# The product of a layer-1 block behind the next block's sums, and at most five gathers in flight

## The chip, the cores and the metric

The kernel runs on one core of a Trainium2 chip. The time is the device time of one execution in microseconds (us). Three runs of the kernel before gave 2042.39, 2044.34 and 2052.66, a median of 2044.34. One more execution was profiled.

The engines of the core are named as in the profile: PE (TensorE, matrix products), DVE (VectorE), ACT (ScalarE), POOL (GpSimd, which here mostly issues gathers and scatters), SP (SyncE, which only issues plain transfers). Each engine has its own queue of instructions and works through it in order; engines wait for one another on semaphores.

## The reference, cut to what matters

```python
def _L1_gnn_ref(input, adj, W, a1, a2):
    h = input @ W
    f1 = h @ a1
    f2 = h @ a2
    e = leaky_relu(f1 + f2.T, negative_slope=0.2)
    scores = where(adj > 0, e, NEG)
    attention = softmax(scores, axis=1)
    return relu(attention @ h)

x = _layernorm(x + layer0(x, adj, ...))
x = _layernorm(x + _L1_gnn_ref(x, adj, W, a1, a2))
```

Two graph-attention layers follow each other over 2708 nodes with 1024 features, both with a residual and a layer norm. The adjacency matrix is sparse: a bit under 0.6% of it is ones. Layer 0 has the same shape with other scores (`relu(f @ g.T)`); the change leaves it as it is.

## The kernel before

**Lists.** The kernel first turns each row of the adjacency matrix into a list of neighbours (up to line 449). The nodes are ordered by the number of neighbours and cut into 22 blocks of 128 (the one numbered 0 holds what is left over). A block has up to four groups of 32 nodes, and each group's lists are cut into tiles: a tile holds 128 neighbour rows, four for each of the 32 nodes. In layer 1 the blocks run in the order of their tile counts: 3, 15, 15, 16, 16 and then 17 blocks of 20 tiles, 405 in all. The text counts them as k = 0 to 21.

**Layer 0** (lines 774 to 1009) leaves its normed output in two DRAM tensors: `X1S`, for the residual, and the table `T1` (`T` in the profile), whose rows are the 1024 features and four more columns, the first of which is the score term f2. A row is 1028 floats, so that a gather of 128 rows moves 526,336 bytes.

**Layer 1** (lines 1012 to 1126) uses that attention @ (x W) = (attention @ x) W: it first sums the gathered rows with the attention's weights and then multiplies the sum of the block by the weight matrix M, which stays in SBUF. For a block k:

- *Gathers.* POOL issues one indirect DMA for each tile into a ring of 32 slots (20 in `ring`, 12 in `more`). The class `Layer` (line 642) keeps the order. A slot is gathered into again once the sums have read it. This happens at three marks inside `Layer.sums`: after 4 tiles, after 12, and after the last. At each mark the gathers for all slots freed since are put into POOL's queue together.
- *Scores.* `scores1` on DVE picks the f2 column out of the landed tiles, adds f1, applies the leaky ReLU and the mask; `Layer.soft` takes the maximum, has ACT do the Exp, and builds `st`, the weights spread into 128x32 matrices, and `rs`, their sums.
- *Sums.* `Layer.sums` runs small matmuls on `rs` (their reciprocal is `ri`), then for each tile two half-width matmuls with a 128x32 weight into the PSUM tile `po`, four column groups of the array side by side. In the profile they read `po<-ring,st 128*32` and `po<-more,st 128*32`, and a block of 20 tiles has 40 of them, which the profile records as some 80. Then ACT scales the sums: `y<-po,ri`, two instructions.
- *Turn and product.* `turn` (line 517) transposes y on PE with eight transposes (`pt<-ident,y`) and ACT copies them to `yT`. `product` (line 535) multiplies `yT` by M in 32 recorded matmuls (`pm<-M,yT`) into the PSUM tile `pm`. For block 0, which has few rows, `split_product` puts four parts of the product side by side in column groups of the array and adds them with a second product.
- *Close.* `close1` loads the residual with SP's queue, adds the ReLU of `pm` to it on DVE (`z<-pm` or `u2b<-pm`, the two buffers of the result), norms it (`bst`, `newton` and so on; ACT's `z<-z,sh,rstd`), and scatters it to the output on POOL. The scatter is issued by a *hook*: the function handed to the next block's `sums` with a tile's number, here 6.

The order of work on each engine is the program order: the wrapper `InOrder` (line 61) ties every instruction to the one before it on its engine, and a scheduler may not move it. Dependencies through tiles become semaphore waits. Each gather or scatter of POOL takes one of eight DMA semaphores in turn, and so waits for the one eight back.

So before the change the PE order in layer 1 is: sums(k), transposes(k), product(k), rs(k+1), sums(k+1). ACT's order is y(k), the yT copies(k), Exp(k+1), z(k). Accumulators in PSUM are one `po`, two `pm` and two `pt`.

Of the kernel before, what the change touches and what calls it, by code (L numbers as in the profile page):

```python
# [106 lines left out]
def listed_path(ctx, tc, x, adj, Wf, bf, Wg, bg, W, bW, W1, a1, a2, out):  # L107

    nc = tc.nc
    P = 128  # L110
# [3 lines left out]
    TW = D + 4  # L114
    NB = (N + P - 1) // P
# [62 lines left out]
        nc.gpsimd.memset(t, 0.0)  # L178

    def gather(engine, dst, table, idx, rows=N):  # L180
        engine.indirect_dma_start(
            out=dst, out_offset=None, in_=table,
            in_offset=bass.IndirectOffsetOnAxis(ap=idx, axis=0), bounds_check=rows - 1, oob_is_err=False)

# [350 lines left out]
    def product(n, xT, w, row=None):  # L535


        pm = ps_m.tile([P, H, 512], F32, name="pm")
        for h in range(H):
            half_product(pm, h, n, xT, w, row)  # L540
        return pm
# [9 lines left out]
    def two_products(n, xT, w, row=None):  # L551

        halves = [ps_m.tile([P, H, 512], F32, name="pm") for h in range(H)]
        for h in range(H):
            half_product(halves[h], h, n, xT, w, row)
        return halves
# [23 lines left out]
    def whole(steps):  # L580

        while True:
            try:
                next(steps)
            except StopIteration as end:
                return end.value
# [54 lines left out]
    class Layer:  # L641

        def __init__(self, units, rings, width, table, stp, batched):
            self.units, self.table, self.width, self.stp, self.batched = units, table, width, stp, batched

            self.first = {g: i for i, g in enumerate(g for u in units for g in u.gs)}
            self.slots = [(t, i) for t in rings for i in range(t.shape[1])]
            self.count = len(self.slots)  # L650
            self.order = [(u, g, t) for u in units for _, g, t in u.tiles]
            assert all(self.first[g] < NSL0 for _, g, _ in self.order[:self.count])
            self.next, self.free, self.most = 0, set(), len(self.order)
# [9 lines left out]
        def gathers(self, latest=None):  # L663
            ready = []
            while self.next < min(self.most, len(self.order)) and (self.next < self.count or self.next - self.count in self.free):
                ready.append(self.next)
                self.next += 1
            if latest is not None and latest + self.count in ready:
                ready.remove(latest + self.count)
                ready.insert(0, latest + self.count)  # L670
            for m in ready:
                u, g, t = self.order[m]
                idx = SL[:, g, t:t + 1] if m >= self.count else SL0[:, self.first[g], t:t + 1]
                gather(pool, self.rows(m), self.table, idx)

        def soft(self, u):

# [97 lines left out]
    with ExitStack() as s0s:  # L775
# [155 lines left out]
        for k, u in enumerate(units):  # L931
            nxt = units[k + 1] if k + 1 < len(units) else None
            b = u.b
# [77 lines left out]

    with ExitStack() as s1s:
        new_pool = lambda name, bufs: s1s.enter_context(tc.tile_pool(name=name, bufs=bufs))
        tp, yp, zp, ovp = (new_pool(n, 1) for n in ("tp1", "yp1", "zp1", "ovp"))
        stp = new_pool("stp1", 2)

        x1 = [rb, u1b]
        z1 = [u2b, zp.tile([P, D], F32, name="z1")]
        more = new_pool("ring1", 1).tile([P, R1 - R0, TW], F32, name="more")

        order1 = sorted(range(NB), key=lambda b: (sum(TILES[g] for g in groups[b]), b))
        units = cut(R1, Q, order1)
        lay = Layer(units, [ring, more], TW, T1[:, :], stp, True)
        done1 = {b: i for i, b in enumerate(order1)}
        for u in units:
            g, at = u.gs[0], lay.first[u.gs[0]]
            if u.at < lay.count:
                dve.tensor_scalar(SL0[:, at:at + u.G], SL[:, g:g + u.G, :], float(N - 1), None, op0=ALU.min)


        fq = ovp.tile([P, NB, Q], F32, name="fq")
        f1q = ovp.tile([P, NB, Q], F32, name="f1q")
        dve.tensor_tensor(fq, f1.unsqueeze(2).to_broadcast([P, NB, Q]), quad.unsqueeze(1).to_broadcast([P, NB, Q]),
                          op=ALU.mult)
        pt = ps_t.tile([P, 4, P], F32, name="pt")
        pe.matmul(pt[:, 0, :Q * NB], rep, fq.rearrange("p b q -> p (b q)"), start=True, stop=True)
        dve.tensor_copy(f1q.rearrange("p b q -> p (b q)"), pt[:, 0, :Q * NB])

        def scores1(u):
            for k, g in enumerate(u.gs):  # L1040
                at = [lay.slots[(u.at + m) % lay.count] for m, tile in enumerate(u.tiles) if tile[0] == k]
                t0 = 0
                while t0 < len(at):

                    t, s = at[t0]
                    step = at[t0 + 1][1] - s if t0 + 1 < len(at) and at[t0 + 1][0] is t else 0
                    c = 1
                    while step > 0 and t0 + c < len(at) and at[t0 + c][0] is t and at[t0 + c][1] == s + c * step:
                        c += 1
                    dve.tensor_scalar(u.sc[:, k, t0:t0 + c], t[:, s:s + (c - 1) * step + 1:max(step, 1), D],  # L1050
                                      f1q[:, u.b, k:k + 1], None, op0=ALU.add)
                    t0 += c
            dve.scalar_tensor_tensor(u.sc, u.sc, SLOPE, u.sc, op0=ALU.mult, op1=ALU.max)
            dve.tensor_add(u.sc, u.sc, masked(u))
            lay.soft(u)

        def close1(b, pm):
            m, xt, z = valid[b], x1[done1[b] % 2], z1[done1[b] % 2]
            sp.dma_start(xt[:m], X1S[start[b]:start[b] + m, :])
            last = b == order1[-1]  # L1060

            def add(h):
                c = slice(h * 512, (h + 1) * 512)
                dve.scalar_tensor_tensor(z[:m, c], pm[h][:m, h, :], 0.0, xt[:m, c], op0=ALU.max, op1=ALU.add)

            if not last:
                dve.scalar_tensor_tensor(z[:m], flat(pm)[:m], 0.0, xt[:m], op0=ALU.max, op1=ALU.add)
            for _ in norm(z, m, add if last else None):
                pass
            yield  # L1070
            scatter(out, ids[:m, b:b + 1], z[:m])


        over = ovp.tile([P, NG, QT], F32, name="over")

        def mark_over(b):

            for g in groups[b]:
                if g == 0:
                    for q in range(Q):  # L1080
                        pool.memset(over[32 * q:32 * q + valid[0], 0, TILES[0]:], 1.0)
                elif TILES[g] < QT:
                    pool.memset(over[:, g, TILES[g]:], 1.0)

        def count_over():
            dve.scalar_tensor_tensor(over, SL, float(N), over, op0=ALU.is_lt, op1=ALU.mult)
            dve.tensor_reduce(bad[:, 0:1], over, AX.XY, ALU.add)
            dve.tensor_reduce(bad[:, 0:1], bad, AX.X, ALU.add)
            pt = ps_t.tile([P, 4, P], F32, name="pt")
            pe.matmul(pt[0:1, 0, 0:1], bad[:, 0:1], ones, start=True, stop=True)  # L1090
            act.copy(flag, pt[0:1, 0, 0:1])

        lay.gathers()
        pool.memset(over, 0.0)
        scores1(units[0])
        closing = iter(())
        for k, u in enumerate(units):
            b = u.b
            po = ps_s.tile([P, H, 512], F32, name="po")
            y = yp.tile([P, D], F32, name="y1")  # L1100
            lay.sums(u, po, {6: [lambda s=closing: [None for _ in s]]}, y)
            yT = tp.tile([P, KC, P], F32, name="yT")
            for _ in turn(y, nrows[b], yT, halves=True):
                pass

            if k + 1 == NB:
                prod = two_products(P, yT, M)
            elif b > 0:
                prod = product(P, yT, M)
            else:  # L1110
                prod = whole(split_product(yT, M, z1[1]))
            for i in (2 * k, 2 * k + 1):
                if i < NB:
                    mark_over(i)
            if k == NB // 2 + 1:
                count_over()
            if k + 1 < NB:
                scores1(units[k + 1])
            closing = close1(b, prod)
            if k + 1 < NB:  # L1120
                next(closing)
            if k + 2 == NB:
                unfit = nc.values_load(flag[0:1, 0:1])
        for _ in closing:
            pass
    return unfit

# [362 lines left out]
```

## Time and profile before

| | |
|---|---|
| median of three runs | 2044.34 us (2042.39 to 2052.66) |
| profiled execution | 2036.4 us, span in the trace 2034.6, mean granted PE clock 0.902 |
| layer 1 in it | from about 1220 us to the end |
| busy in the span: PE, DVE, ACT, POOL | 1634.2, 1169.8, 641.6, 1193.3 us (80, 57, 32, 59%) |
| mean DMA rate | 247 GB/s |
| layer 1's gathers | 260 into `ring`, mean 1002 ns on POOL, and 145 into `more`, mean 999 ns |
| product with M in layer 1 (`pm<-M,yT`) | 704 matmuls, 327.5 us |
| the sums of both layers (`po<-ring,st`) | 2660 matmuls, 333.5 us |
| ends of the sums of k = 4, 5, 20, 21 | 1360.67, 1389.74, 1971.12, 2003.47 us |

A line of the profile's timeline gives the start, the duration, the engine, the source line (here that of a helper, L71, for all), the operation, what it writes and reads, the shapes, the number of instructions taken together, and in brackets the engine's idle time before it and what ended it. "remote" or "another core or an unknown queue" means that the wait's releaser could not be found in the records. Of a waits list the columns are the total, the number of waits and the longest. A stretch of the windows table gives, for each engine, the busy time and the number of instructions, and then the granted PE clock (1.00 is full), the mean busy share of the 16 DMA engines, and the rate.

### The profile page before, as it was taken

Reading aid. Unit: us, or ns where it says so; the run is one execution under the profiler, and the core shown is the slowest. Engines: PE = TensorE matmul, PEld = TensorE weight load, DVE = VectorE, ACT = ScalarE, POOL = GpSimd, SP = SyncE. Lnnn points to the kernel's source line nnn. Section 1 sums busy time; section 2 is a strip of 40 time slices with the busy share of each in tenths; the row PEclk is TensorE's granted clock in tenths of the full one; section 3 lists DMA queues with packets and bytes.
Section 4 is the critical chain, followed back from the end, with each engine's and each line's share of the span. In section 5 each row is a group of like instructions: output and inputs, shape, how many; then the busy total and the mean of one; then the engine's idle time right before and its main releaser. Section 6 shows DMA issues by size and latency. Waiting matters only on the chain.

```text
span 2034.6 us, 22766 instructions
## 1 busy us (share of the span) xinstructions
PE 1634.2 (80%) x7313; PEld 686.3 (34%) x7313; DVE 1169.8 (57%) x3539; ACT 641.6 (32%) x861; POOL 1193.3 (59%) x1192
## 2 busy tenths in 40 slices
PE   5998569889999999999999963887657776657766
PEld 3443223333434434443434420332223232223222
DVE  6879447867878888888888751332231332222322
ACT  4545326444444455544455410110110110110110
POOL 7877545746656667666666416655555555555540
PEclk9999779989989999999999986998878878878878
DMA  7644545746867668877678728877788778888760
GB/s 276 242 170 149 179 159 206 268 165 249 300 239 284 243 234 280 295 283 279 232 245 297 300 97 340 297 274 287 261 294 279 266 266 290 278 279 286 261 222 23
DMA packets 149981, 502.25 MB, mean 247 GB/s; under 512 B 32468, under 2 KB 32500, under 8 KB 147144
## 3 DMA queue, kind: packets, MB, share of 16 engines
q0 software_dynamic: 132032, 427.76, 59.5%
q1 hardware_dynamic: 10202, 55.72, 7.5%
q10 hardware_dynamic: 7618, 17.23, 2.4%
q8 instruction: 59, 0.97, 0.2%
q14 instruction: 70, 0.57, 0.1%
HBM read 509.64 MB, written 33.75 MB: 267 GB/s over the span
## 4 chain that ended last, share of the span: by engine, by line
PE 21%; DVE 9%; another core or an unknown queue 9%; issue 7%; DMA 2%; POOL 2%; ACT 2%; ACTq 1%; POOLq 0%; DVEq 0%
PE pm L71 17%; DVE j L71 2%; PE pt L71 2%; PE po L71 2%; DVE newton L71 2%; DVE bst L71 1%; POOL ring L71 1%; DVE rstd L71 1%; DMA ring<-T,SL 1%; DVE z L71 1%; ACT y L71 1%; DMA ring<-in_x_dram,SL 1%; ACTq L71 1%; DVE u2b L71 1%
## 5 line engine op out<-in xcount | busy, mean ns | idle before, releaser
L71 POOL DMA_INDIRECT ring<-in_x_dram,SL x405 | 437.6, 1081 | 308.7 <-issue 97.3
L71 DVE SCALAR_TENSOR_TENSOR j<-ring,Fr 128x1024 bf16<-128x1024 f32 x402 | 495.2, 1232 | 95.3 <-DMA ring<-in_x_dram,SL 61.0
L71 POOL DMA_INDIRECT ring<-T,SL x260 | 260.6, 1002 | 207.8 <-PE po L71 111.0
L71 ACT COPY Fr<-pm 32x1024 f32<-32x1024 f32 (+2 forms) x353 | 340.8, 965 | 20.9 <-issue 11.9
L71 PE MATMUL pm<-M,xT 128*128 128x512 f32 x672 | 323.8, 630 | 22.1 <-issue 22.0
L71 PE MATMUL po<-ring,st 128*32 128x512 f32 x2660 | 333.5, 606 | 0.2 <-PE pt L71 0.2
L71 PE MATMUL pm<-M,yT 128*128 128x512 f32 (+1 forms) x704 | 327.5, 644 | 6.3 <-issue 4.2
L71 PE MATMUL pm<-Wt,xT 128*128 128x512 f32 (+1 forms) x704 | 305.3, 599 | 3.4 <-issue 3.2
L71 PE MATMUL pt<-ident,y 128*128 128x128 f32 (+1 forms) x352 | 62.7, 334 | 202.1 <-ACT y L71 188.2
L71 POOL DMA_INDIRECT more<-T,SL x145 | 144.9, 999 | 117.4 <-PE po L71 64.8
L71 PEld LDWEIGHTS pm<-M,yT 128*128 128x128 f32 (+1 forms) x704 | 138.2, 204 | 183.2 <-issue 177.6
L71 PEld LDWEIGHTS pm<-M,xT 128*128 128x128 f32 x672 | 130.6, 199 | 200.0 <-issue 200.0
L71 PEld LDWEIGHTS pm<-Wt,xT 128*128 128x128 f32 (+1 forms) x704 | 124.7, 186 | 157.6 <-issue 157.0
L71 PEld LDWEIGHTS po<-ring,st 128*32 128x32 f32 x2660 | 98.1, 112 | 185.4 <-issue 185.0
L409 POOL TENSOR_TENSOR adj<-adj,iota 128x2708 f32<-128x2708 f32 (+3 forms) x23 | 130.5, 5684 | 24.1 <-ACT adj L71 24.0
L71 ACT ACTIVATE y<-po,ri 128x512 f32<-128x512 f32 (+1 forms) x88 | 55.9, 684 | 250.1 <-remote 166.9
L71 ACT ACTIVATE scores<-scores 128x24 f32<-128x24 f32 (+5 forms) x44 | 10.0, 227 | 390.4 <-DVE scores L71 234.2
L71 PEld LDWEIGHTS pt<-ident,y 128*128 128x128 f32 (+1 forms) x352 | 50.5, 172 | 236.2 <-ACT y L71 208.6
L412 DVE MAX8 cand<-adj 128x8 f32<-128x136 f32 (+2 forms) x440 | 97.3, 285 | 36.5 <-POOL adj L409 36.5
L71 ACT ACTIVATE z<-z,sh,rstd 128x1024 f32<-128x1024 f32 (+1 forms) x31 | 38.5, 1241 | 245.1 <-DVE sh L71 244.9
L71 PE MATMUL pm<-halfT,WfT 128*128 128x512 f32 x256 | 113.9, 600 | 1.1 <-ACT WfT L71 1.1
L71 DVE TENSOR_SCALAR scores<-ring,f1q 128x4 f32<-128x4 f32 (+4 forms) x98 | 21.3, 240 | 155.5 <-DMA ring<-T,SL 124.1
(201 smaller groups left out, 1490.7 us busy)
## 6 DMA issues: line engine op xcount, KB each, us to landing
adj<-in_adj_dram SPq DMA_DIRECT2D x21, 1354.0 KB
X1S<-z SPq DMA_DIRECT2D x19, 512.0 KB
ring<-in_x_dram,SL POOLq DMA_INDIRECT x405
u1b<-X1S SPq DMA_DIRECT2D x11, 512.0 KB
rb<-X1S SPq DMA_DIRECT2D x10, 512.0 KB
ring<-T,SL POOLq DMA_INDIRECT x260
rows<-in_L_gnn_Wg_dram ACTq DMA_DIRECT2D x8, 512.0 KB
rows<-in_L_gnn_Wf_dram ACTq DMA_DIRECT2D x8, 512.0 KB
```

Of the source, the lines that this page charges most:

```text
L71: made = self.tc.keep_in_program_order(op(*args, **kwargs))
L409: nc.gpsimd.tensor_tensor(k[:n, cut], k[:n, cut], iota[:n, cut], op=ALU.mult)
L412: nc.vector.max(cand[:n, s, :], k[:n, s * SEG:min((s + 1) * SEG, N)])
```

## The change

Two things change, both in layer 1 alone.

1. *The order.* The product of a block is issued behind the next block's sums. PE's order becomes sums(k), product(k-1), transposes(k), rs(k+1), sums(k+1). `yT` is kept from one iteration to the next in the dictionary `turned`, and its pool has two buffers. `next(steps)` issues the transposes; the yT copies on ACT now come behind `scores1(k+1)`, so behind the Exp. `close1(k-1)` follows that. The scatter's hook moves from tile 6 to tile 12 of the sums, which puts it behind the gathers of the second mark in POOL's queue, and it belongs to the block before. Block 0 (k = 0) still runs its split product in its own iteration. After the loop come the product of k = 21 and the closings of the last two blocks; the product of k = 20 has come behind the sums of k = 21.
2. *The limit.* `Layer` has a new argument `flight`, 5 for layer 1 and none for layer 0. Every gather gets a dependency on the gather five ahead of it, so that POOL waits until that one has landed before it issues the next.

The number of instructions on each engine is the same.

```diff
@@ class Layer
-        def __init__(self, units, rings, width, table, stp, batched):
+        def __init__(self, units, rings, width, table, stp, batched, flight=None):
+            self.flight, self.issued = flight, []
...
-                gather(pool, self.rows(m), self.table, idx)
+                made = gather(pool, self.rows(m), self.table, idx)
+                if self.flight is not None:
+                    if len(self.issued) >= self.flight:
+                        tc.add_manual_dep(
+                            made.ins, self.issued[-self.flight],
+                            mybir.DependencyInfo(mybir.DependencyClass.Sync, mybir.DependencyReason.DATA),
+                            reason="gathers in flight")
+                    self.issued.append(made.ins.name)
@@ layer 1
-        tp, yp, zp, ovp = (new_pool(n, 1) for n in ("tp1", "yp1", "zp1", "ovp"))
-        stp = new_pool("stp1", 2)
+        yp, zp, ovp = (new_pool(n, 1) for n in ("yp1", "zp1", "ovp"))
+        stp, tp = (new_pool(n, 2) for n in ("stp1", "tp1"))
...
-        lay = Layer(units, [ring, more], TW, T1[:, :], stp, True)
+        lay = Layer(units, [ring, more], TW, T1[:, :], stp, True, 5)
...
+        turned = {}
         for k, u in enumerate(units):
...
-            lay.sums(u, po, {6: [lambda s=closing: [None for _ in s]]}, y)
+            lay.sums(u, po, {12: [lambda s=closing: [None for _ in s]]}, y)
+            closing = iter(())
+            prods = {c: product(P, turned.pop(c), M) for c in list(turned)}
             yT = tp.tile([P, KC, P], F32, name="yT")
-            for _ in turn(y, nrows[b], yT, halves=True):
-                pass
-
-            if k + 1 == NB:
-                prod = two_products(P, yT, M)
-            elif b > 0:
-                prod = product(P, yT, M)
+            steps = turn(y, nrows[b], yT, halves=True)
+            next(steps)
+            if b == 0:
+                for _ in steps:
+                    pass
+                prods[b] = whole(split_product(yT, M, z1[1]))
             else:
-                prod = whole(split_product(yT, M, z1[1]))
+                turned[b] = yT
...
+            if k + 1 < NB:
+                scores1(units[k + 1])
+            for _ in steps:
+                pass
             if k == NB // 2 + 1:
                 count_over()
-            if k + 1 < NB:
-                scores1(units[k + 1])
-            closing = close1(b, prod)
-            if k + 1 < NB:
+            for c, pm in prods.items():
+                closing = close1(c, pm)
                 next(closing)
...
+        prod = two_products(P, turned.pop(b), M)
         for _ in closing:
+            pass
+        for _ in close1(b, prod):
             pass
```

More of the change, by code (lines that the diff above doesn't have):

```diff
@@ L180, in gather @@
     def gather(engine, dst, table, idx, rows=N):
-        engine.indirect_dma_start(
+        return engine.indirect_dma_start(
             out=dst, out_offset=None, in_=table,
```

## The prediction

> **What bounds the kernel now.** All times are microseconds. I read the page's slices first: PE is 0.6 to 0.7 busy and DMA 0.7 to 0.8 in the last 16 slices, which are layer 1 (1220 to 2035), so neither is full there. Then the waits between 1700 and 1990, whose columns are us in all, times, longest:
>
> ```profile
> ACT y L71 <- remote: 104.8, 8, 14.1
> PE pt L71 <- ACT y L71: 95.2, 8, 12.8
> DVE scores L71 <- DMA ring<-T,SL: 50.7, 13, 11.3
> POOL ring L71 <- PE po L71: 37.1, 4, 9.5
> POOL more L71 <- PE po L71: 30.8, 3, 10.5
> ```
>
> In each 20-tile block PE waits 12 to 13 us for y, the scaled sums, and POOL waits 9 to 10 us for PE. Then the timeline of one block (start, us, what ran):
>
> ```profile
> 1883.09 1.23 DVE L71 SCALAR_TENSOR_TENSOR z<-pm,u1b 128x1024 f32<-128x1024 f32 x1 [12.72 <-PE pm L71]
> 1883.13 5.76 PE L71 MATMUL po<-ring,st 128*32 128x512 f32 x51
> 1885.34 0.99 POOL L71 DMA_INDIRECT ring<-T,SL  x1 [9.00 <-PE po L71]
> ...
> 1890.00 2.07 PE L71 MATMUL po<-more,st 128*32 128x512 f32 x16
> ...
> 1895.77 0.99 POOL L71 DMA_INDIRECT ring<-T,SL  x1 [0.31 <-issue]
> ...
> 1900.96 0.99 POOL L71 DMA_INDIRECT ring<-T,SL  x1 [0.30 <-issue]
> ...
> 1902.86 0.23 DVE L71 TENSOR_SCALAR scores<-ring,f1q 128x4 f32<-128x4 f32 x1 [0.80 <-DMA ring<-T,SL]
> ...
> 1904.02 1.27 ACT L71 ACTIVATE y<-po,ri 128x512 f32<-128x512 f32 x2 [13.81 <-remote]
> 1904.21 0.99 POOL L71 DMA_INDIRECT more<-T,SL  x1 [2.26 <-remote]
> 1904.76 1.97 PE L71 MATMUL pt<-ident,y 128*128 128x128 f32 x8 [12.69 <-ACT y L71]
> ...
> 1907.56 0.83 DVE L71 TENSOR_TENSOR st<-scores,stack 128x640 f32<-128x640 f32 x1 [1.65 <-ACT scores L71]
> ```
>
> The last sum ends at 1892.07, yet y starts at 1904.02, 11.95 later, with ACT idle. In 13 of the 17 20-tile blocks the lag is 11.9 to 12.1; in the last, with no gather running, 0.12. POOL issues gathers back to back until 1901.95, and the release comes 2.0 after that, for POOL's next gathers too. I read it as: the completion signal of the sums' column-tiled matmuls (128*32) is held while POOL issues gathers and let go in its first pause. Whether PE itself stands still meanwhile is what matters, so I asked for busy time in five stretches of this block (busy and count by engine, then granted clock, DMA share, GB/s):
>
> ```profile
> 1883.10:1892.10 9.00, 8.97 (x96) 2.63 (x94) 5.51 (x19) 1.24 (x1) 5.23 (x6) 1.00 0.67 204
> 1892.10:1897.00 4.90, 0.00 (x0) 0.00 (x0) 0.00 (x0) 0.00 (x0) 3.75 (x4) 1.00 0.97 368
> 1897.00:1904.70 7.70, 0.00 (x0) 0.00 (x0) 2.69 (x16) 0.68 (x2) 4.46 (x5) 0.50 0.93 329
> 1904.70:1910.50 5.80, 5.74 (x13) 3.40 (x14) 2.01 (x8) 1.94 (x6) 4.58 (x5) 0.50 0.90 299
> 1868.50:1883.00 14.50, 14.50 (x35) 6.29 (x35) 0.91 (x2) 0.77 (x3) 6.12 (x6) 0.96 0.80 285
> ```
>
> The clock falls to 0.50 five us into the gap, as for an idle array. And layer 0's timeline has the wanted order: its sums end at 1067.6, PE runs transposes and a product from 1067.59 to 1076.4, while that block's y waits until 1074.03. So the gap can be filled. The chain per block is now sums 8.94, lag 11.95, y 0.74, transposes 1.97, product 14.5, rs 0.15 = 38.25; the ends of the sums from k=4 to k=20 give 610.45/16 = 38.15.
>
> **The change part by part.** The sum is made against the profiled execution, 2036.4 (span 2034.6 plus 1.8), 7.9 under the median of 2044.34; I move the result by 8 at the end.
>
> *Product behind the next sums.* Instruction counts do not change, only order. PE then runs sums(k), product(k-1), transposes(k), sums(k+1): 8.94 + 14.0 to 14.5 + 1.1 (row at full clock 1.24, at half 1.97) + 0.15 = 24.2 to 25.6. The lag of 11.95 and y's 0.74 lie beside the product, which needs neither; 14.0 covers 12.7. Without that cover the block is back at 38. PE stops being the bound by 12.6 to 14 a block; what is late next?
>
> (1) Scores. From the start of the sums (1883.13) to the last tile of the next block (1902.86) is 19.7, then 3.0 to the Exp's input, Exp and st: 1908.4 less start = 25.3. The Exp now stands ahead of the yT copies (1.24) and the scatter no longer stands between the gathers of mark 4 and mark 12 (1.33), so 23 to 25.3.
>
> (2) POOL. Gathers are 1.297 apart (0.99 and 0.30): 20 of them 25.9, scatter 1.33, one pause of 2.26 in which the signal comes: 29.5; without the pause 27.3.
>
> (3) DMA. A block moves 20 gathers of 526,336 B, a residual load and a scatter of 512 KB each: 11.56 MB. At 368 GB/s (share 0.97, above) 31.4; at 329, 35.1; at 400, which the layer's first 40 us show, 28.9. Share times period says the same: 0.81 x 38.3 = 31.0.
>
> (4) *The wait of a gather for the fifth ahead.* No trace shows it. The gather issued at 1895.77 is read at 1902.86, some 7.0 later. Five in flight then allow one per (7.0 + 0.3)/5 = 1.46, so 20 x 1.46 + 1.33 = 30.5, and most of the pause of 2.26 is spent while gathers drain. Ends of the term: it never binds (29.5 stays), or latency grows as the DMA fills, to 8.5, 1.76 a gather, 36.5. Little's count bears the middle: 368 GB/s x 7.0 = 2.58 MB, or 4.9 gathers in flight already. Behind a waiting gather stand scatters and later gathers in POOL's queue; nobody waits for the scatter, and the scores wait is in (1).
>
> I take the nearest row of a full DMA, T = 31.3, with ends 27.3 and 36.5. The Trainium skill's page "DMA: Bandwidth & Descriptors", section "Anatomy of one DMA — SWDGE (gpsimd) path", gives a fixed 2.0 us plus bytes over 436 GB/s for one such transfer, 3.2 here; five in flight at that would be 0.64 each, and an estimate from it alone has the limit never bind, as in rival (d). The 7.0 above says that transfers queue behind one another, and the row decides.
>
> 16 periods x (38.15 - 31.3) = 110 saved.
>
> *The short blocks, k=1 to 4* (15 to 16 tiles, 27.4 each): 15.5 gathers and two 512 KB transfers, 9.2 MB, 25 at 368 GB/s: 2 saved each, 8 (0 to 12).
>
> *k=0* keeps its inline product. Its column-tiled matmuls end at 1241.2 but ACT's copy starts at 1265.56, after POOL's 35 gathers. With the limit the POOL may pause earlier and let that go: 0 to 20 saved, or, if the first 35 gathers slow from 1.297 to 1.46, 6 lost. At 400 GB/s (share 1.02) the DMA is the limit either way, so 0.
>
> *Clock.* A product after a 12.7 us gap starts at half clock (8 matmuls in 5.68 of the 14.55); with the gap filled that is gone, 0.5 a block, hidden under the DMA. The Trainium skill's page "TensorE: Matmul & The Clock Gate", section "What's actually happening", puts the fall to half at about 3.4 us of idle; the trace agrees in kind with 4.9. By that rule a gap left at 31.3 - 25 = 6 would still throttle part of the block.
>
> *The tail.* Before, sums(20) end to the span's end is 63.5. After, the product of 20 comes behind the last sums: product(19) 14.2, transposes, rs, sums(21) 10.2, product(20) 14, turn 1.8, product(21) 14.0, closing 14.9 (2019.75 to the end) = 69. So 5 lost.
>
> *bufs, hook 12, z.* Two yT buffers cost no instruction. z(k-1) is normed (1883.09 to 1890.2, 7 us) after scores(k+1), as now, and its scatter stands behind mark 12's gathers, at least 10 us after z is done; if z were late, POOL would wait with 8 gathers behind it, and 10 us is the cover.
>
> Sum: -110 - 8 + 5 = -113: 1923 on the profiled basis, **1931** on the median's.
>
> **The rivals.**
> (a) *POOL is the bound*: the DMA takes what POOL gives, as in the first 40 us (400 GB/s at 1.297). T = 27.3 to 29.5: 16 x 8.65 to 10.85 = 138 to 174, and 8 to 20 more at k=0 to 4: 1860 to 1900. Against: scattered dips to 299 GB/s beside a residual load.
> (b) *The gap cannot be filled*: the sums truly run late under the gathers, and the profile's modelled ends are wrong; the product then comes later by as much: T about 8.9 + 12 + 14.5 + 1.5 = 37, 18 saved, 5 lost: 2025 to 2040. Against: the clock at 0.50 and layer 0.
> (c) *Slower: the limit of five starves the DMA.* Place: POOL's queue. It decides against the change where a gather's cadence exceeds (38.15 - 1.33)/20 = 1.84, that is a latency of 8.9 between issue and the POOL seeing it landed. At 10, T = 20 x 2.06 + 1.3 = 42.5, 16 x 4.4 = 70 slower, and 65 gathers at k=0 to 4 lose 0.5 each: 2145; at 9.2, 2075. For: 7.0 is only what DVE saw, and the row at 299 GB/s would make it 8.8. Against: five already fly, and a limit on flight shortens the queue.
> (d) *The limit changes nothing*, only the order acts: T of the DMA alone, 31.0 to 31.4. It gives the forecast's time.
>
> **How the numbers follow.** Forecast with (d) 0.52, 1890 to 1965 (T 29 to 33.5); (a) 0.16; a limit that costs half, T 33.5 to 37.5, 1965 to 2030, 0.13; (b) 0.09; (c) 0.10. The range leaves out (c) and the lower part of (a): 1875 to 2032. A measurement of this kernel tells some 0.5%, 10 us, from no change. Faster: 0.52 + 0.16 + 0.13 + half of (b) = 0.85; same 0.05; slower 0.10.
>
> **What would show it.** In the changed kernel's trace: y's wait of 12 us stays or shortens, but PE's wait for y vanishes and a product starts within 0.2 of the last sum; the ends of the sums stand 31 apart; DMA share in a block rises from 0.8 to 0.95; POOL's 9 us wait for PE becomes short waits for a DMA of the ring; the granted clock in layer 1 rises. The prediction is wrong if the product is recorded 12 us behind the sums (b), if gathers are over 1.84 apart (c), or if the scores' chain, not the gathers, sets a period well over 31.

## The result and the profile after

The changed kernel took 1943.22 us (median of four runs, 1916.32 to 1952.93) against 2048.5 before (median of four, 2042.39 to 2083.75), a ratio of the medians of 0.949. Taken over the runs in the faster of the two states that executions show, 1916.32 and 1940.62 against 2042.39, 2044.34 and 2052.66, the ratio is 0.942, 95% interval 0.927 to 0.958: faster by some 5.8%. The forecast was 1931 with a range of 1875 to 2032. The execution that was profiled is the longest of the four, 1952.93 (span 1951.1), so its sum is made against the profiled 2036.4 of before: 83.5 saved, of the 113 that were forecast.

From the ends of the sums in the two traces:

| stretch | before | after | difference | forecast |
|---|---|---|---|---|
| start to the end of sums(0) | 1232.7 | 1241.1 | +8.4 | (not touched) |
| sums(0) to sums(1) | 45.8 | 44.1 | -1.7 | 0 |
| sums(1) to sums(4) | 82.2 | 75.7 | -6.5 | -8 |
| sums(4) to sums(20), 16 blocks | 610.4 | 522.5 | -88.0 | -110 |
| sums(20) to the end | 63.5 | 67.8 | +4.3 | +5 |

The first row is no effect that this pair can show: a second trace of the kernel before, below, has 1240.5 there.

A 20-tile block fell from 38.15 to 32.65, not to 31.3. The windows table has the 16 blocks in one row (busy and count of PE, PEld, DVE, ACT, POOL, then granted clock, DMA share, GB/s), the first of before, the second of after:

```profile
1360.70:1971.10 610.40, 421.98 (x2178) 174.54 (x2178) 166.40 (x692) 62.01 (x113) 337.68 (x391) 0.84 0.79 275
```

```profile
1360.80:1883.30 522.50, 420.43 (x2181) 167.58 (x2179) 166.94 (x692) 61.73 (x113) 334.28 (x388) 0.90 0.90 319
```

The same work in 88 us less. But the DMA's share is 0.90, not the 0.95 that the prediction gave as its sign, and PE is busy for 420 of 522. The waits of after between 1600 and 1900 say what stands in the way now:

```profile
ACT y L71 <- remote: 65.3, 5, 16.3
ACT yT L71 <- remote: 36.8, 5, 10.7
...
PE pt L71 <- ACT yT L71: 29.1, 8, 11.4
...
POOL ring L71 <- DMA ring<-T,SL: 5.5, 9, 1.8
```

PE's wait for y (up to 12.8) is gone, as forecast. A new one stands in its place: the small rs matmuls of the next block (`pt<-rs`) wait up to 11.4 for the yT copies. POOL's wait for the fifth gather ahead is small: the four rows of that list that name a gather come to 12.6 us. One long block in the timeline, k = 8:

```profile
1485.21 14.00 PE L71 MATMUL pm<-M,yT 128*128 128x512 f32 x32
...
1486.45 1.26 ACT L71 ACTIVATE y<-po,ri 128x512 f32<-128x512 f32 x2 [7.45 <-issue]
...
1499.05 1.04 PE L71 MATMUL pt<-ident,y 128*128 128x128 f32 x8
...
1507.62 0.99 POOL L71 DMA_INDIRECT ring<-T,SL  x1 [0.30 <-issue]
...
1511.20 1.23 DVE L71 SCALAR_TENSOR_TENSOR z<-pm,u1b 128x1024 f32<-128x1024 f32 x1 [7.02 <-remote]
1511.29 1.14 ACT L71 COPY yT<-pt 128x512 f32<-128x512 f32 x3 [8.12 <-remote]
1511.93 0.39 PE L71 MATMUL pt<-rs,stack 128*32 128x1 f32 x16 [11.84 <-ACT yT L71]
...
1516.09 0.99 POOL L71 DMA_INDIRECT ring<-T,SL  x1 [7.13 <-PE po L71]
```

The product starts with the last sum (1485.28). Product and transposes end at 1499.2 and 1500.1, the weights of the next block are ready at 1504.2. But both DVE's read of the product and ACT's copies start at 1511.2, together, 2.6 after the last gather of POOL's run ended (1507.62 + 0.99). So not only the column-tiled sums' signal is held while POOL issues: those of a full product and of transposes are, and here they come in one moment. The rs matmuls need a `pt` buffer, there are two, both hold transposes until the yT copies are done, and so the next sums wait for that moment. POOL in turn waits 7.13 for these sums to free its slots. Blocks 14 and 18, whose transposes were signalled at once, took 26.6 and 26.4 from the start of one sums to the next; blocks 5, 6, 8, 10, 13, 15 and 16, where the copies started 4 to 11 behind them, 32 to 40. Block 20 was signalled at once too and took 30.6, since its sums alone took 15.4.

A pause of POOL is not the whole rule. In the same block 8 y follows its sums by 1.17 while POOL issues every 1.30. In the trace of before, block 5 has y 7.40 behind the sums and the yT copies 3.60 behind the transposes, block 12 has y 3.61 behind, and POOL paused before none of the three.

The timeline gives the whole 32.65, as means over the 16 blocks: rs and sums 11.77 (9.25 in the trace of before, by the same count), product 14.00 less an overlap of 0.07, from there to the end of the transposes 1.70, and 5.25 until the next rs. The sums themselves, 8.9 in most blocks of before, take 10.1 to 15.4. Part of that is the clock, granted at 0.50 from 1511.9 to 1515.5 behind the wait of 11.84, and part is time in which a matmul starts late with no wait named.

### The profile page after: what moved, and what is told of

It reads as the page before. It is cut to its first block, busy times and chain, and to the rows that moved or that the text cites. A ratio compares the mean times of both kernels' runs of the same rounds, so it can differ in the third digit from the quotient of the medians.

```text
span 1951.1 us, 22749 instructions
## 1 busy us (share of the span) xinstructions
PE 1632.2 (84%) x7313; PEld 680.0 (35%) x7313; DVE 1174.6 (60%) x3539; ACT 641.5 (33%) x861; POOL 1196.5 (61%) x1192
## 5 line engine op out<-in xcount | busy, mean ns | idle before, releaser
L71 PE MATMUL po<-ring,st 128*32 128x512 f32 x2660 | 363.5, 627 | 7.7 <-issue 6.3
L71 PE MATMUL pm<-M,xT 128*128 128x512 f32 x672 | 316.1, 621 | 14.0 <-issue 14.0
L71 PE MATMUL pm<-M,yT 128*128 128x512 f32 (+1 forms) x704 | 299.1, 596 | 1.5 <-issue 1.1
L71 PEld LDWEIGHTS pm<-M,yT 128*128 128x128 f32 (+1 forms) x704 | 126.8, 186 | 172.6 <-issue 172.1
L71 PEld LDWEIGHTS po<-ring,st 128*32 128x32 f32 x2660 | 106.6, 115 | 208.0 <-issue 204.3
L71 PE MATMUL pt<-rs,stack 128*32 128x1 f32 x680 | 14.6, 182 | 134.2 <-ACT yT L71 77.2
L71 PE MATMUL po<-more,st 128*32 128x512 f32 x580 | 107.8, 692 | 0.8 <-issue 0.8
L71 POOL DMA_INDIRECT SL<-LD,idq x85 | 88.1, 1036 | 25.8 <-issue 24.9
```

Source lines behind the costliest of these rows:

```text
L71: made = self.tc.keep_in_program_order(op(*args, **kwargs))
```

## The experiments

The runs went to several chips, and the chip turned out to matter more than any edit. The time of the kernel before was 2048 to 2072 (medians) where the first result was taken and on the chips numbered 15, 13 and 9, and 1764.5 and 1765.6 on chips 4 and 3. I call the first kind *holding*, the second *prompt*. Every time below stands beside the kernel before on the same chip.

### The two parts, and the place of rs, on a prompt chip

The order alone is the changed kernel with the limit off:

```diff
-        lay = Layer(units, [ring, more], TW, T1[:, :], stp, True, 5)
+        lay = Layer(units, [ring, more], TW, T1[:, :], stp, True)
```

> The changed kernel without the limit of five; only the order. Theory H (the changed trace suggests it): PE's completion signals, of the products and transposes too, are held while POOL issues gathers without a break of about 2 us, and come together after it. In the changed kernel the next block's rs matmuls wait for the yT copies, and these for the transposes' held signal (yT 0.6 to 11.2 after the transposes' end), so a block lasts as long as POOL's run: 20 x 1.30 + 1.33 + 2 + 5.5 until the next gather = 35. Without the limit there are fewer breaks, so every block is of that kind: 35 to 36 a block against 32.65, 1975 to 2005 on a median of 2045. Rival G (a block lasts as long as its transfers take, and the limit only delays gathers): 30 to 32 a block, 1905 to 1940.

The limit alone is the kernel before with `flight` as in the change and 5 for layer 1; nothing else.

> The kernel before with the limit of five alone. H: the waits of POOL for a landed gather are breaks in which the sums' signal comes through, so y's lag of 11.9 gets shorter in some blocks, to 6 on average as in the changed kernel: 1960 to 2030. G and my prediction's rival (c): the lag stays and gathers come later: 2040 to 2060.

And the changed kernel with another place for rs:

```diff
-            pt = ps_t.tile([P, 4, P], F32, name="pt")
+            pt = ps_m.tile([P, H, 512], F32, name="pm") if self.batched else ps_t.tile([P, 4, P], F32, name="pt")
             place = lambda k, h: 32 * ((k + 2 * h) % 4)
```

> The changed kernel with the rs matmuls of layer 1 written to a buffer of pm instead of one of the two pt buffers, so that sums(k+1) no longer wait for the yT copies. H: the long blocks (33 to 40) fall to those of the blocks whose transposes were signalled at once (26.4 to 29.2): 28 to 30 a block, 1870 to 1905. G: nothing changes, 1930 to 1950.

Measured on chip 4, against 1764.54 before: order alone 1775.81, ratio 1.0065 (1.0042 to 1.0087); limit alone 1817.24, 1.0311 (1.0287 to 1.0336); the changed kernel with rs moved 1827.81, 1.039 (1.034 to 1.0441). All are slower, the first by less than 2%. None of the expectations was met, because their ground was gone: in the traces y comes 0.05 to 0.14 after the last sum in every block of the three kernels, with POOL issuing all the while. No signal is held there.

What the chip shows instead looks at first like the bound that I had forecast from. Windows of the 16 blocks, order alone first, limit alone second:

```profile
1266.00:1706.00 440.00, 395.90 (x2183) 162.02 (x2180) 165.83 (x693) 60.56 (x114) 335.73 (x399) 0.96 0.99 381
```

```profile
1265.00:1752.00 487.00, 408.37 (x2178) 161.26 (x2178) 167.69 (x693) 62.54 (x113) 339.42 (x402) 0.94 0.95 347
```

Without the limit a block takes 27.5 (439.8/16 from sums(4) to sums(20)), POOL's 27.3 of the prediction's item (2), and the DMA gives 381 GB/s. With the limit it takes 30.46 (487.3/16), and POOL's largest row of waits for a landed gather, 3.8 us between 1300 and 1743 with the order alone, comes to:

```profile
POOL ring L71 <- DMA ring<-T,SL: 25.5, 43, 2.1
```

All four rows that name a gather come to 51.4 against 7.1, which is 3 us a block and the difference of the two block times. Item (4) had 30.5 for the limit. So on this chip, where nothing else hides it, the limit costs what was worked out.

In the first of the two windows the DMA's share is 0.99, so it does not tell a bound by transfers from one by POOL's cadence; the small gathers below do. Both windows and both of the first result's move the same amount, 10.4 to 10.6 MB a block (381 GB/s x 440 us / 16 is 10.48, 275 x 610.4 / 16 is 10.49), not the 11.56 MB of the prediction's item (3).

### The same bytes from another queue

The kernel before, with layer 1's gathers after the first 32 as plain transfers from SP, which leaves out the gathering of the right rows:

```diff
-                gather(pool, self.rows(m), self.table, idx)
+                if self.batched and m >= self.count:
+                    r = P * (m % (N // P))
+                    sp.dma_start(self.rows(m), self.table[r:r + P, :self.width])
+                else:
+                    gather(pool, self.rows(m), self.table, idx)
```

> The kernel before, but layer 1's gathers after the first 32 are plain transfers of 128 consecutive rows, same bytes, issued by SP. It leaves out the gathering of the neighbours' rows there. If POOL's issuing holds the signals: y's lag falls from 11.9 to under 1 and the block from 38.2 to 25.5 to 29: 1840 to 1900. If the DMA traffic holds them: the lag stays over 5 and the time within 2010 to 2050.

It ran once, on the same prompt chip: 1830.31, and blocks of 25 to 35. This decides nothing. There was no lag to remove, and the new lags of 0.1 to 8.5 in it have a plain cause: SP's queue now has the residual's load behind 20 transfers, so the z of the block before is late, and it stands ahead of y in ACT's order (z at 1405.93, y at 1407.08 in block 8).

### The kernel before and the changed one again, elsewhere

> The kernel before itself, for its trace beside the next run. In the runs with the order alone, the limit alone and rs in pm, the time before was 1764.5, not 2044, and y came 0.1 us after the sums in every block. If PE's signals are held on some chips and not on others: where the time is near 1765, y's lag is 0.1 and a block is sums 8.8 + 0.1 + 0.75 + transposes 1.3 + product 14 + rs 0.15 = 25 to 26.5; where it is near 2045, the lag is 12 in most blocks and a block is 38. If something else makes the 280 us, the lag is 12 at either time.

> The changed kernel itself beside it. Where the lag is 0.1: there is no gap for the product to fill, the limit of five costs as in the run of the limit alone (29.7 a block) and the tail 5: 1815 to 1850 against 1765, 2.8 to 4.8% slower. Where the lag is 12: 4 to 7% faster, as measured first. If the signals are no property of the place: faster by 4 to 7% at either time.

Chip 15 holds: before 2054.64 (this profiled run 2044.28), changed 1938.24 (median of five, 1921.61 to 1957.08), ratio 0.947 (0.919 to 0.976). The verdict on record is unclear, though the interval lies under 1. In the trace of before y's lag is 11.6 to 12.1 in 13 of the 17 long blocks again, in that of the changed kernel a block takes 32.0 (512.3/16). So the first result repeats in size, and the lag goes with the time of the kernel before, in all runs.

### Small gathers

POOL issues as many gathers, but 16 bytes a row, which leaves out the transfer of the rows:

```diff
-                gather(pool, self.rows(m), self.table, idx)
+                if self.batched and m >= self.count:
+                    few = self.table.rearrange("n w -> (n w)")[:N * 4].rearrange("(n w) -> n w", w=4)
+                    gather(pool, self.rows(m)[:, :4], few, idx)
+                else:
+                    gather(pool, self.rows(m), self.table, idx)
```

> The kernel before, but layer 1's gathers after the first 32 fetch 4 columns a row instead of 1028, from a small table: POOL issues as many gathers, with next to no bytes. It leaves out the transfer of those rows. On a chip where the time before is near 2045: if POOL's issuing holds PE's signals, y's lag stays near 12 in the 20-tile blocks and the time within 2010 to 2045; if the moved bytes hold them, the lag falls under 1, a block to 25.5 and the time to 1840 to 1870. Where the time before is near 1765 the lag is 0.1 and only the bytes' own share shows: 1735 to 1765.

> The changed order without the limit, and with the rs matmuls in a buffer of pm, so that the next sums wait neither for the limit nor for the transposes' signal. Where the signals are held: POOL waits for the sums' signal at the third mark, which is a break, so y comes 21 after the sums' start and the block takes POOL's 20 x 1.30 + 1.33 + 2 = 29.5: 1880 to 1915 against 2045 (the changed kernel: 1940). Theory G: no better than the changed kernel, 1930 to 1950. Where they are not held: as the order alone, 0.3 to 1.0% slower than 1765.

Chip 3 is prompt (before 1765.58). Small gathers: 1749.85, with y's lag at 0.07 to 0.17 and 20-tile blocks of 25.1 to 28.8. The 16 us are all that the bytes cost there. Blocks 6 to 12 take 25.1, which is PE's chain without the lag. Blocks 15 to 20 take 27.3 to 28.8, five of the six 27.3 or 27.4, with the DMA nearly idle (share 0.15, 41 GB/s) and POOL's 106 instructions filling the whole window at 1.30 each:

```profile
1554.00:1691.00 137.00, 129.93 (x681) 48.80 (x680) 49.33 (x211) 19.03 (x36) 105.00 (x106) 1.00 0.15 41
```

So once the lead of the 32 slots is used up, POOL's cadence sets the block, bytes or no bytes, at the 27.3 of the prediction's item (2), and a product moved behind the sums has nothing left to fill. The order with rs moved and no limit: 1778.62, ratio 1.0076 (1.0051 to 1.010), as the order alone, so the place of rs costs nothing and the 3.9% above are order and limit. Whether POOL's issuing or the moved bytes hold the signals on the other chips was not tried there.

### The order and rs on a holding chip

> The order alone again, for a chip on which PE's signals are held (time before near 2045; on the two chips where it is near 1765 they are not). Theory H there: 35 to 36 a block, since without the limit POOL has fewer breaks in which the transposes' signal comes: 1960 to 2005. G: 30 to 32 a block, 1905 to 1940. Where they are not held: 0.4 to 0.9% slower, as measured.

> The changed kernel with the rs matmuls in a buffer of pm, again for such a chip. H: the sums no longer wait for the yT copies; the long blocks of 33 to 40 fall to 27 to 31: 1870 to 1905. G: as the changed kernel, 1925 to 1950. Where the signals are not held: 3.4 to 4.4% slower than 1765, as measured.

> The changed kernel beside them, on the same chip. Where the signals are held: 1915 to 1957 as before. Where they are not, it has not run yet: order alone and limit alone cost 0.65% and 3.1% there, so 3 to 4.5% slower, 1815 to 1845, with the lag at 0.1.

Chip 13, before 2065.4: order alone 1948.44, ratio 0.9445 (0.9363 to 0.9526); changed with rs moved 1947.61, 0.9427 (0.9319 to 0.9535); changed 1957.23 (four runs, 1921.39 to 1971.55), by the medians 0.948, with no interval. No difference among the three is resolved. The order alone is enough for the gain, and the limit neither adds nor takes anything that these runs can show; the limit alone was not run on a holding chip. My H was wrong in both numbers: the order alone fell between the ranges of H and G, rs moved into G's. The traces say why.

In the order alone the blocks do not all turn long, they alternate. Read off the timeline (us from the start of a block's sums; the yT copies, and the next sums):

```
k              9     10     11     12     13    ...   16     17     18     19
transposes   26.6   38.4   26.2   37.3   26.6        27.0   30.6   27.0   37.9   (end)
yT starts    26.5   38.0   26.6   38.0   27.3        26.6   37.8   26.6   37.8
next sums    27.3   38.8   27.4   39.4   28.1        27.4   38.7   27.4   38.6
gathers        16     24     16     24     16          15     25     15     25
```

A short block has 15 or 16 gathers issued in it and leaves the next one 24 or 25, which its transposes, or their signal, have to sit through; in some of the long blocks the transposes themselves end late. The mean is 32.85 a block, that of the changed kernel on this chip 32.56.

With rs moved the next rs no longer wait for yT, and PE creeps in its place: it starts a few matmuls, stands, and starts a few more. From the transposes' end to the next rs it is 2.2 on average, 4.3 in the changed kernel on this chip, but rs and sums grow from 12.7 to 14.8. The worst place is between blocks 19 and 20:

```profile
1856.16 1.25 PE L71 MATMUL pt<-ident,y 128*128 128x128 f32 x8
1857.34 0.19 PE L71 MATMUL pm<-rs,stack 128*32 128x1 f32 x1
...
1858.41 0.24 PE L71 MATMUL pm<-rs,stack 128*32 128x1 f32 x4 [0.88 <-issue]
...
1859.84 0.28 PE L71 MATMUL pm<-rs,stack 128*32 128x1 f32 x4 [1.19 <-issue]
...
1864.86 3.65 PE L71 MATMUL po<-ring,st 128*32 128x512 f32 x14 [1.24 <-issue]
1865.64 1.23 DVE L71 SCALAR_TENSOR_TENSOR u2b<-pm,rb 128x1024 f32<-128x1024 f32 x1 [10.63 <-remote]
1865.70 1.14 ACT L71 COPY yT<-pt 128x512 f32<-128x512 f32 x3 [11.63 <-remote]
```

The 16 rs matmuls, 0.3 us in most blocks, take 6 us here in steps of up to 1.4, with no wait named, and the sums behind them run on at about the time when the held signals come. So there was no slack behind the wait for yT: a block is 32.2 without it and 32.6 with it.

### Breaks in POOL's run, in the old order

The last run puts the theory to use: the order of before, no limit, and two places where POOL must stand still.

```diff
-            return (4, 12, tiles) if self.batched else range(1, tiles + 1)
+            return (4, tiles) if self.batched else range(1, tiles + 1)
...
+        lay.most = len(units[0].tiles) + len(units[1].tiles)
         lay.gathers()
         pool.memset(over, 0.0)
...
-                prod = whole(split_product(yT, M, z1[1]))
+                split = split_product(yT, M, z1[1])
+                next(split)
+                lay.most = len(lay.order)
+                lay.gathers(behind=pe.last)
+                prod = whole(split)
```

(`behind` gives the first of these gathers a dependency on that instruction of PE.)

> The kernel before in its own order, without a limit, with two breaks put into POOL's run: the freed slots are gathered into at two marks (after 4 tiles and after the last) instead of three, so that POOL stands still when the sums end; and of the first 32 gathers 18 are issued at once and the rest waits for block 0's column-tiled product. If a break of 2 us is what lets PE's signals through: on a chip that holds them (time before near 2045) y's lag falls from 12 to 0 to 5, the block from 38.2 to 30 to 31.5 (POOL: 20 x 1.30 + 1.33 and two breaks of 2), and sums(0) to sums(1) from 46 to 25 to 30: 1885 to 1925, faster than the changed kernel. If the signals come with the amount of outstanding transfers or at random, the lag stays near 12 on average or the block at 36 to 39: 1980 to 2045. On a chip that does not hold them: the gathers of the old second mark come 4 us later, POOL's 27.3 a block against about 26.6: 0 to 1.5% slower.

Chip 9, holding (before 2071.85): 1946.6, ratio 0.9422 (0.9343 to 0.9501); the verdict on record is unclear, though the interval lies under 1. The theory's mark is met: y's lag is 0.1 to 0.9 in 15 of the 16 blocks from k = 5 to 20, most of which had 12, without the product moved at all.

```profile
1726.30 1.27 ACT L71 ACTIVATE y<-po,ri 128x512 f32<-128x512 f32 x2 [4.47 <-PE po L71]
1726.49 1.02 POOL L71 DMA_INDIRECT more<-T,SL  x1 [1.49 <-PE po L71]
```

The sums end at 1725.37 in POOL's pause, and y starts 0.9 later. A block takes 31.40 (502.4/16), and sums(0) to sums(1) fell from 45.8 to 29.0, both within what was expected. The total missed the expected 1885 to 1925, for two reasons in the trace. The gathers now run beside the sums, and PE creeps there too, so the sums take 11 to 16 instead of 8.8:

```profile
1745.02 0.59 PE L71 MATMUL po<-more,st 128*32 128x512 f32 x1 [0.62 <-issue]
...
1746.42 0.59 PE L71 MATMUL po<-more,st 128*32 128x512 f32 x1 [0.81 <-issue]
...
1749.28 7.35 PE L71 MATMUL po<-ring,st 128*32 128x512 f32 x64 [0.84 <-issue]
```

And of the 17 us gained at block 0, 14 went back at block 1, whose y waits 16.7 behind the 29 gathers put off: sums(1) to sums(2) takes 41.7 instead of 27.5. It does not beat the changed kernel; it reaches the same ratio by taking the lag away instead of filling it.

## Why the prediction was right, and where not

*The gap can be filled: right.* PE takes up the product at the last sum in every block, before's wait for y is gone, and the granted clock of the 16 blocks rises from 0.84 to 0.90. Rival (b) is out, and the order alone gives the gain (0.9445 on chip 13). Two of the signs named did not come: the DMA's share reached only 0.90, and POOL's wait for PE stayed, 7.13 behind block 8.

*What is held: wrong.* I read the hold as one of column-tiled matmuls only. The product's and the transposes' signals are held as well (1511.20 and 1511.29 above). In the trace of before the copies start with the transposes in every block but block 5, where they start 3.60 behind their end: that one place could have warned.

*The term that was mis-sized* is T = 31.3, from a full DMA at 368 GB/s. A block took 32.65, 32.0 and 32.6 in three traces, at a DMA share of 0.90 in the first: the chain there is POOL's run of gathers, the signal after it, the yT copies, rs, and the next sums. The step that missed it is the one on "bufs, hook 12, z", which said that two yT buffers cost no instruction and left out that the copies, now behind the product's end, free the two `pt` buffers that rs needs. The new wait came to 29.1 us in eight waits between 1600 and 1900. Taking it away alone gained nothing measurable (0.9427 beside 0.948 by medians, with an interval wider than that), since the sums took up its place. They are the second thing left out: the sum has 8.94 for them, and they took 11.57 on average in the 16 blocks.

*The bytes: wrong, and the number was in part luck.* A gather does not move 526,336 bytes, except for the first 32. The lists are padded with indices outside the table, and the kernel's gather leaves such rows out (`bounds_check`); only for the first 32 are they brought into the table. The packed trace of before has 46,726 packets of one row (4112 bytes) for the 405 gathers, whose 128 rows each would be 51,840. With the 10.49 MB a block of its windows row, 368 GB/s gives 28.5, not 31.3, and the sum would have come out some 45 lower, near 1886. So a count of bytes that was too high made up for most of the wait that was missing, and the 12 us between forecast and median say little for the working.

*DMA as the bound: wrong also where nothing is held.* There a block of the same order took 27.5 at 381 GB/s, and blocks with next to no bytes took 27.3 as well: rival (a), POOL's cadence, for which I had given 0.16.

*The limit of five: its size right, its place wrong.* 30.5 worked out, 30.46 measured on a prompt chip; on a holding chip no cost of it is resolved (0.9445 without it, 0.948 by medians with it). By the Trainium skill's page "DMA: Bandwidth & Descriptors", section "Anatomy of one DMA — SWDGE (gpsimd) path", the estimate was that it never binds; the run of the limit alone, 3.1% slower, differs, and it decides.

*Tail, short blocks, block 0:* 67.8 for 69, -6.5 for -8, -1.7 for 0.

*What the prediction could not see* is that its ground, the lag of 12, is not there on every chip. On a prompt chip order alone is 0.65% slower and, with the limit and rs moved, 3.9%. The changed kernel itself was not run on one; by these, an estimate, it would be 3 to 4% slower there. That is rival (c)'s side and its mechanism, far under the latency of 8.9 that (c) asked for: without the lag a block of before takes some 27 (an estimate: 26.4 on average with small gathers, and the 16 us of the bytes over 21 blocks), not 38, and the limit's 30.5 is above that.

## What to carry to other kernels

A wait whose releaser finished long ago (here 12 us) is worth a question of its own: is it the work, or only its signal, that is late? Before costing a reorder that hides it, list every other signal of that engine that the new order puts into the same stretch, and every buffer that each of them frees. And where a gain rests on such a lag, time the kernel before on a second chip first: here 2050 or 1765 decides, by the runs of its parts, the sign of the change. And count the bytes that a gather with padded lists really moves in the trace's own rate before calling the DMA a bound.

## What was not expected of the hardware

- The same kernel takes 1764.5 to 1765.6 on two chips, and 2048 to 2072 on three others and where the first result was taken. On the slower ones PE's completion signals take effect up to 12 us late while POOL issues gathers 1.30 apart, in most blocks some 2 to 3 us after POOL stops, in some without a pause; on the faster ones 0.1 after the matmul beside the same gathers. Breaks in POOL's run took the lag away (0.1 to 0.9), but whether the signals leave late or are taken late, whether the issuing or the bytes do it, and whether it belongs to the chip or to a condition it was in, stays open.
- In the same stretches PE itself slows to a few matmuls every 1.4 us (rs in the run with rs moved, the sums in the last run). What it waits for is not recorded, and no run tells that apart. PE is not alone: in block 8 above DVE's four copies `mq<-m` take 1.9 (1500.26 to 1502.17), 0.9 elsewhere, with no wait named between them.
- The recording itself differs between the two kinds, and this rival is untested. In the eight traces of the holding kind the packed trace has 1447 to 1578 updates of DVE's semaphore for 2101 to 2109 instructions that make one; in the six of the prompt kind 1985 to 2111 for 1993 to 2109, at most 8 short. For PE it is 558 to 579 of 598 or 617 against all but 3 at most. So on the holding chips records are lost, and the load that loses them may be what holds the engines, or both may have one cause. Every run on record has a granted clock beside its time, so none is known to have gone without recording.
